# Two recurrences stepped in turns instead of in lockstep, with finer interleaving of side work, in a four-layer hybrid block

## The chip, the core and the metric

The program runs on one core of one Trainium2 chip. The metric is the device time of one execution in microseconds (us). A core has these engines, each with its own in-order instruction queue: TensorE (PE, matrix multiplication into PSUM), VectorE (DVE), ScalarE (ACT), GpSimd (POOL) and SyncE (SP, which here only issues DMA transfers). POOL also issues DMA transfers, the indirect ones, whose rows are chosen by indices in memory. An instruction that waits for another engine holds up everything behind it on its own engine. Nothing but such waits ties the engines together.

## What is computed

Input x is 4 sequences of 512 tokens of 128 features, all in float32. Four layers follow one another, each as `x = x + layer(layernorm(x))`:

```python
x = x + attn_a(layernorm(x), W)                   # 16 heads, scores |q.k|**2 with cumulated gates
x = x + ffn(layernorm(x), gate_w, bias, w1,w2,w3) # 8 experts, 2 per token, hidden 352
x = x + attn_b(layernorm(x), Wi, Wf, Wg, ..., Wo) # gated recurrence
x = x + ffn(layernorm(x), gate_w, bias, w1,w2,w3) # the same expert layer again
```

The recurrence layer projects x three times, runs a causal convolution of four taps over two of the projections, and then, per feature, scans over time; its output is normalized, gated and projected:

```python
f = sigmoid(conv(x @ Wf));  i = silu(conv(x @ Wi)) * (1 - f)
h_t = f_t * h_(t-1) + i_t
y = (h * rsqrt(mean(h*h) + eps) * g_norm * silu(x @ Wg)) @ Wo
```

The expert layer sends each token to its two best experts of eight: `silu(x @ w1[e]) * (x @ w3[e]) @ w2[e]`, weighted by the score.

## The kernel before

**Halves and stages.** After the attention the four sequences are worked as two halves q = 0, 1 of two sequences. The expert layer occurs twice, as generations gen = 1 and 2. Its tokens are sorted by expert into NS = 23 blocks of 128 places. So there are four expert stages (gen, q), in the order (1,0), (1,1), (2,0), (2,1), each a call of `blocks` (L982) with 28 iterations j. Block j is worked over several iterations: `first` (L1002) multiplies by w1 and w3 (tile ph, L1020; four matmuls), ACT takes silu (sl, L1027), DVE multiplies (h, L1028). Two iterations later `turn_and_second` (L1032) transposes h on PE (L1040) and ACT copies it (hT, L1053). Two iterations after that, PE multiplies by w2 (L1046) and ACT copies the result (yb, L1056). One iteration later `send` (L1058) writes the rows to memory at yg by an indirect DMA on POOL (L1059). Every fourth block `turn_x` (L990) transposes four blocks of fetched rows (px, L994; xT, L998). `fetch` (L962) brings rows eight blocks ahead: for stage (1,0) by SP, for the others by an indirect DMA on POOL (L970).

**Side work.** While one half is in the expert stage, the other half's connecting work is woven in. It is written as Python generators ("streams"); each `yield` ends a piece, and the block loop asks for the next piece at fixed points by `next(side)`. Since all engines are in-order, where a piece is asked for is where its instructions stand in every queue. Per iteration there are `points` such points: one after `first`, one at the end, and, if points > 2, one between the transposes and the w2 matmuls. A piece that issues a fetch reports "dma", and the rest of that iteration's points are dropped. `skip(n)` makes n empty pieces, to let time pass between a producer and its consumer. The list of stages, points and side streams is at L1229.

**The side streams.** Beside (1,0) runs the routing of half 1: `route` (L685) normalizes (stats, apply, turn), multiplies by the gate weights (pl, L747), finds the two best experts by a chain of small DVE operations (L773 to L806), counts places on PE (pp, L819 and L821), derives each token's place (L827 to L897) and inverts the list by counting matches (hit, L911; pi, L904). Then `begin` (L975) fetches the first eight blocks. Beside (1,1) and (2,0) runs `then` (L1212): `combine` (L1087) loads the expert results (yk) and adds them to x (L1102), `hgrn` (L1118) is the recurrence layer, then come `route` and `begin` for generation 2. Beside (2,1) only `combine` with the store of the output runs, and after the last block once more.

**Lockstep.** The two sequences of a half run through `combine` and `hgrn` under `both` (L220): each piece holds the same step of both sequences. `route` then normalizes both with tiles that hold the whole half.

**PSUM.** The tiles ph, px and all PE results of the side work come from one ring of three buffers (`ring`, L209), so an allocation waits until the third last one has been read. `busy` (L256) are matmuls without use that keep PE occupied; one stands before the last matmuls of each recurrence.

**The attention.** It runs in 16 steps (b, g) with the next two steps overlapped; POOL multiplies the scores by the decay (`faded`, L505, L514). From the middle on, the routing of half 0 is a side stream there too, at four points per step (`point`, L595); it ends with 16 indirect DMA writes of rows ("puts", L868) on POOL. What is left of it and `begin(1, 0)` is run off before the first block, one `busy` matmul to a piece.

## Time and profile before

| what | value |
|---|---|
| median of 14 runs | 636.79 us (633.35 to 649.2) |
| profiled execution, its own time | 633.89 us |
| span from first to last instruction of it | 632.2 us |
| mean granted TensorE clock | 0.921 |
| attention up to the first block's matmul | 0 to 255.3 us |
| stage (1,0), 23 blocks and routing of half 1 | 255.3 to 326.4 us |
| stage (1,1), with recurrence and routing of half 0 | 326.4 to 438.1 us |
| stage (2,0), with recurrence and routing of half 1 | 438.1 to 552.3 us |
| stage (2,1), with the sums and store of half 0 | 552.3 to about 616 us |
| last sums and store of half 1 | about 616 to 632.2 us |

How to read the profile: a page gives busy time by engine and, by groups, each line's instructions. The timeline lists instructions in order of time: start, busy time, engine, line, operation, tile written <- tiles read, count, and in square brackets the idle time of the engine before it and what released it. "PEclk" is the TensorE clock that was granted, in tenths. "remote" as releaser means that the profile could not tell which event ended the wait. Stage borders in the table are the starts of the first ph matmul of each stage in the timeline.

### The profile page before, as it was taken

The page shows a single profiled execution, that of the slowest core. Times are in us where ns is not written, and L with a number is a line of the kernel's source. Part 1 is how long each engine was busy: PE and PEld are TensorE (multiplying, and loading weights), DVE is VectorE, ACT ScalarE, POOL GpSimd, SP SyncE. Part 2 cuts the span into 40 slices and gives each one's busy share as a digit, 9 for nine tenths or more (in the row PEclk, how much of TensorE's full clock was granted, in tenths as well). Part 3 has the DMA queues.
Part 4 walks back from the last instruction along what each step waited for, and adds up shares of the span by engine and source line. Part 5 has one row for each costly group of instructions (what it writes and reads, how often), then busy time and mean ns, then how long its engine had stood idle before and what let it go on. Part 6 is the DMA issues. An engine that isn't in the chain of part 4 may idle for free.

```text
span 632.2 us, 11339 instructions
## 1 busy us (share of the span) xinstructions
PE 528.2 (84%) x4065; PEld 349.2 (55%) x4065; DVE 323.6 (51%) x772; ACT 281.9 (45%) x507; POOL 338.7 (54%) x487
## 2 busy tenths in 40 slices
PE   9899999999988978799886989774798978589890
PEld 4345555556554545567664567553556755457570
DVE  5527668796869754473216445640634655033211
ACT  2446776777755650443432434431343433134350
POOL 4645748566744696035674228347522733756651
PEclk9889999999988998999989979996897988699995
DMA  2360008993000001161122001301200121123113
GB/s 79 106 198 4 8 2 107 141 147 17 2 2 2 14 32 43 39 131 35 38 64 70 18 14 38 94 27 46 93 17 17 31 77 39 47 76 108 43 37 111
DMA packets 53974, 34.96 MB, mean 55 GB/s; under 512 B 18040, under 2 KB 49040, under 8 KB 53920
## 3 DMA queue, kind: packets, MB, share of 16 engines
q1 hardware_dynamic: 48052, 22.49, 18.1%
q0 software_dynamic: 5664, 11.70, 6.3%
q8 instruction: 34, 0.56, 0.4%
q14 instruction: 20, 0.16, 0.1%
q10 hardware_dynamic: 204, 0.05, 0.0%
HBM read 16.56 MB, written 17.66 MB: 54 GB/s over the span
## 4 chain that ended last, share of the span: by engine, by line
PE 53%; DVE 21%; issue 9%; POOL 7%; ACT 5%; DMA 3%; another core or an unknown queue 1%; SPq 1%; POOLq 0%; DVEq 0%; ACTq 0%
PE ph L1020 11%; PE pb L1046 7%; DVE p L444 6%; PE s L489 5%; PE busy L259 3%; PE pb L1040 3%; PE pd L473 3%; PE pd L470 3%; DVE h L1028 2%; PE od L525 2%; POOL yg L1059 2%; POOL p L514 2%; PE oo L530 1%; ACT sl L1027 1%; DMA yk<-yg 1%
## 5 line engine op out<-in xcount | busy, mean ns | idle before, releaser
L1059 POOL DMA_INDIRECT yg<-yb,xb x92 | 91.4, 994 | 130.1 <-ACT yb L1056 115.7
L1020 PE MATMUL ph<-w,xT 128*128 x368 | 133.6, 489 | 15.1 <-DVE xT L998 5.7
L514 POOL TENSOR_TENSOR p<-p,dec 128x256 f32<-128x256 f32 (+1 forms) x96 | 86.5, 918 | 68.5 <-ACT p L503 64.6
L1028 DVE SCALAR_TENSOR_TENSOR h<-ph,xb,sl 128x352 f32<-128x352 f32 x92 | 53.3, 580 | 130.1 <-ACT sl L1027 98.2
L503 ACT ACTIVATE p<-p,aeps 128x1024 f32<-128x1024 f32 (+1 forms) x96 | 94.1, 1004 | 38.4 <-DVE p L444 34.7
L444 DVE TENSOR_SCALAR p<-s 128x1024 int32<-128x1024 int32 (+1 forms) x96 | 95.2, 1035 | 23.4 <-PE s L489 23.4
L1046 PE MATMUL pb<-w2s,hT 128*128 x552 | 81.4, 286 | 14.3 <-remote 9.9
L1020 PEld LDWEIGHTS ph<-w,xT 128*128 128x128 f32 x368 | 66.5, 200 | 42.3 <-issue 9.0
L1027 ACT ACTIVATE sl<-ph,xb 128x352 f32<-128x352 f32 x92 | 51.5, 560 | 79.8 <-PE ph L1020 51.6
L1053 ACT COPY hT<-pb 128x384 f32<-128x384 f32 x92 | 44.1, 479 | 86.7 <-PE pb L1046 54.6
L1046 PEld LDWEIGHTS pb<-w2s,hT 128*128 128x128 f32 x552 | 72.8, 200 | 17.5 <-ACT yb L1056 13.1
L970 POOL DMA_INDIRECT xb<-xg,from x69 | 67.3, 976 | 25.0 <-issue 13.6
L489 PE MATMUL s<-qT,kT 32*128 32x256 f32 (+3 forms) x512 | 66.4, 476 | 9.8 <-DVE p L444 8.4
L1040 PE MATMUL pb<-ident,h 128*128 128x128 f32 x276 | 47.6, 283 | 7.3 <-ACT yb L1056 4.8
L489 PEld LDWEIGHTS s<-qT,kT 32*128 32x128 f32 x512 | 31.1, 185 | 34.9 <-DVE p L444 18.2
L1040 PEld LDWEIGHTS pb<-ident,h 128*128 128x128 f32 x276 | 35.5, 145 | 26.9 <-issue 13.1
L477 ACT ACTIVATE dec<-pd 128x1024 f32<-128x1024 f32 x32 | 32.5, 1023 | 27.0 <-PE pd L473 27.0
L998 DVE COPY xT<-px 128x512 f32<-128x512 f32 (+1 forms) x24 | 15.9, 660 | 33.8 <-PE px L994 30.5
L530 PE MATMUL oo<-p,vo 128*9 128x128 f32 x768 | 31.2, 279 | 0.0
L470 PE MATMUL pd<-negm,identb 128*128 128x512 bf16 x64 | 25.0, 390 | 5.5 <-DVE p L444 5.5
L461 POOL TENSOR_SCALAR kT<-kf,hsel 128x512 f32<-128x512 f32 x16 | 25.1, 1571 | 7.6 <-DVE kf L374 7.6
L525 PE MATMUL od<-p,v 128*9 128x128 f32 x512 | 24.8, 280 | 3.6 <-POOL p L514 3.6
(238 smaller groups left out, 694.2 us busy)
## 6 DMA issues: line engine op xcount, KB each, us to landing
xg<-zero SPq DMA_DIRECT2D x4, 1472.0 KB
yk<-yg SPq DMA_DIRECT2D x16, 256.0 KB
xg<-xk SPq DMA_DIRECT2D x6, 520.0 KB
w<-in_L_ffn_w_dram SPq DMA_DIRECT2D x2, 1408.0 KB
xb<-xg SPq DMA_DIRECT2D x23, 65.0 KB
yg<-yb,xb POOLq DMA_INDIRECT x92
xb<-xg,from POOLq DMA_INDIRECT x69
x<-in_L_attn_a_x_dram SPq DMA_DIRECT2D x4, 256.0 KB
```

The lines of the kernel that those rows point to most:

```text
L444: nc.vector.tensor_scalar(dst.bitcast(I32), src.bitcast(I32), 0x7FFFFFFF, None, ALU.bitwise_and)
L489: nc.tensor.matmul(sp[hh // 2][:, hh % 2, n : n + tn * P], kT[r, s * P : (s + 1) * P], qT[r, t0 * P : (t0 + tn) * P], start=True, stop=True,)
L503: nc.scalar.activation(pa, pa, AF.Square, bias=aeps)
L514: nc.gpsimd.tensor_tensor(d, d, e, ALU.mult)
L970: nc.gpsimd.indirect_dma_start(out=t, out_offset=None, in_=xg[gen, q], in_offset=bass.IndirectOffsetOnAxis(ap=gots[gen, q][1][:, j : j + 1 ...
L1020: nc.tensor.matmul(ph[:, w, 0:HID], xT[j], w13f[:, bass.ds(reg[j][0] + w * HID, HID)], start=True, stop=True,)
L1027: nc.scalar.activation(sl, ph[:, 0, 0:HID], AF.Silu, scale=score)
L1028: nc.vector.scalar_tensor_tensor(hs_[j % NHB][:, 0:HID], ph[:, 1, 0:HID], score, sl, ALU.mult, ALU.mult)
L1040: nc.tensor.transpose(bank[:, cols], hs_[jt % NHB][:, cols], ident)
L1046: nc.tensor.matmul(py, hT[js][:, k * P : (k + 1) * P], w2f[:, bass.ds(reg[js][1] + k * C, C)], start=(k == 0), stop=(k == len(FCH) - 1),)
L1053: nc.scalar.copy(hT[jt], bank[:, 0:HP])
L1059: put = nc.gpsimd.indirect_dma_start(out=yg[gen, q], out_offset=bass.IndirectOffsetOnAxis(ap=loaded[gen, q, j][:, C : C + 1].bitcast(I32), ...
```

## The change

The diff has these parts.

- `both` becomes `in_turns`: the two sequences' streams alternate piece by piece, the first one four pieces ahead. A stream now holds the sums, the recurrence and also the normalization for the routing (`route_norm`, with tiles of one sequence), so `route` starts behind both. The tiles xk are split by sequence.
- Four side points per iteration in the first three stages: the new one is inside `first`, between the w1 and w3 matmuls. The empty pieces are counted anew.
- `results` loads all four yk tiles at once; the sums come nine pieces later. `combine` only adds.
- The recurrence's steps are cut differently; the `busy` matmul before its last matmuls is dropped; ACT copies the mean squares before DVE reads them.
- In the routing the scores of both choices are taken in one multiply and one reduction, and ACT copies them into the four row tiles; SP writes the rows in four transfers.
- `begin` fetches two blocks per piece (in the slow form one, as before).
- In the last attention step DVE instead of POOL multiplies by the decay, and puts are issued two per point in the last two steps.

```diff
-    def both(*streams):
-        streams = list(streams)
+    def in_turns(first, second, lead):
+
+        for _ in range(lead):
+            next(first, None)
+            yield
+        streams = [second, first]
         while streams:
-            streams = [s for s in streams if next(s, END) is not END]
-            yield
+            for st in tuple(streams):
+                if next(st, END) is END:
+                    streams.remove(st)
+                else:
+                    yield
...
-        def faded(pas, rnd, dec):
+        def faded(pas, rnd, dec, eng):
...
-                nc.gpsimd.tensor_tensor(d, d, e, ALU.mult)
+                eng.tensor_tensor(d, d, e, ALU.mult)
...
-                if piece == "dma" and k % 2:
+                if piece == "dma" and (k % 2 or n + 1 >= NST):
                     next(second, None)
...
+                fader = nc.gpsimd if n + 1 < NST else nc.vector
+                faded(tiles[0], 0, decs[n], fader)
...
+    def route_norm(gen, q, i, early=False):
+
+        nm, xk = f"{gen}_{q}_{i}", xks[q]
+        xn = xk[0][i][:, :, 0:C]
+        yield from normed(xs[seqs(q)[i]], xn, f"r{nm}", 0 if early else 1)
+        xnT = rp.tile([P, NB, P], FP, tag=f"xnT{i}", name=f"xnT_{nm}")
+        turned(xnT.rearrange("p n t -> p (n t)"), xn, nm)
+        nc.scalar.copy(xk[1][i][:, :, 0:C], xn)
+        turned_rows[gen, q, i] = xnT
+        yield
+
+    turned_rows = {}
+
+    def first_done():
+        yield "first"
...
-        stats(0)
...
-            turn(1)
-            yield
+        nm, xk = f"{gen}_{q}", xks[q]
         yield
         pl = ring(f"pl_{nm}")[:, 0, 0 : HT * NE].rearrange("p (n e) -> p n e", e=NE)
         for n in range(HT):
-            nc.tensor.matmul(pl[:, n, :], xnT[:, n, :], gT, start=True, stop=True)
+            xnT = turned_rows[gen, q, n // NB]
+            nc.tensor.matmul(pl[:, n, :], xnT[:, n % NB, :], gT, start=True, stop=True)
...
-        yield
-        if not early:
-            yield
+        yield from skip(1 if early else 3)
...
-        for k, h in enumerate((hot1, hot2)):
-            nc.vector.tensor_tensor(tmp, sc, h, ALU.mult)
-            nc.vector.tensor_reduce(xk[k][:, :, C + 1], tmp, AX.X, ALU.add)
+        nc.vector.tensor_tensor(
+            both_tmp, sc.unsqueeze(1).to_broadcast([P, 2, HT, NE]), both_hot, ALU.mult
+        )
+        score = rp.tile([P, 2, 2, NB], FP, tag="score", name=f"score_{nm}")
+        nc.vector.tensor_reduce(
+            score.rearrange("p k i n -> p (k i n)"),
+            both_tmp.rearrange("p k n e -> p (k n) e"), AX.X, ALU.add,
+        )
+        for k in range(2):
+            for i in range(2):
+                nc.scalar.copy(xk[k][i][:, :, C + 1], score[:, k, i, :])
         for k in range(0 if early else 2):
-            nc.sync.dma_start(
-                out=xg[gen, q][k * HT * P : (k + 1) * HT * P, :].rearrange(
-                    "(n p) c -> p n c", p=P
-                ),
-                in_=xk[k],
-            )
-        yield from skip(1 if early else 4)
+            for i in range(2):
+                r = (2 * k + i) * T
+                nc.sync.dma_start(
+                    out=xg[gen, q][r : r + T, :].rearrange("(n p) c -> p n c", p=P),
+                    in_=xk[k][i],
+                )
+        yield from skip(1 if early else 3)
...
-        yield
+        yield from skip(1 if early else 2)
...
-            yield from skip(1 if m else 3)
+            yield from skip(1 if m else 2)
...
-        yield
+        yield from skip(2)
...
-            for j in range(2 * GR):
+            if not slow:
+                yield from skip(3)
+            for j in range(0, 2 * GR, 2):
                 fetch(gen, q, j)
+                if slow:
+                    yield "dma"
+                    yield
+                fetch(gen, q, j + 1)
                 yield "dma"
...
                 ph = ring(f"ph_{nm}_{j}")
+                dma = False
                 for w in range(2):
+                    if w and points > 3:
+                        dma = next(side, None) == "dma"
                     nc.tensor.matmul(
...
+                return dma
...
-                if j < NS:
-                    first(j)
+                dma = j < NS and first(j)
                 if j % GR == 1 and j // GR + 1 < groups:
                     turn_x(j // GR + 1)
-                dma = next(side, None) == "dma"
+                dma = dma or next(side, None) == "dma"
...
+        def results(gen, q, got):
+
+            yk = {}
+            for i in range(2):
+                for k in range(2):
+                    t = fp1.tile([P, NB, C], FP, tag=f"yk{k}{i}", name=f"yk{k}_{gen}_{q}_{i}")
+                    r = (2 * k + i) * T
+                    ld = nc.sync.dma_start(
+                        out=t, in_=yg[gen, q][r : r + T, :].rearrange("(p n) c -> p n c", n=NB)
+                    )
+                    behind(ld, got[2], "every result is in its row")
+                    yk[k, i] = t
+            return yk
+
+        def combine(q, yk, i, store=False):
+            b = seqs(q)[i]
             for k in range(2):
...
-                nc.vector.tensor_tensor(xs[b], xs[b], yk[k], ALU.add)
-                if not store:
+                nc.vector.tensor_tensor(xs[b], xs[b], yk[k, i], ALU.add)
+                if k or not store:
...
             yield from normed(xs[b], xn, f"h{b}", 1)
-            yield from skip(2)
...
-            pf = ring(f"pf_{b}")
...
+            pr = ring(f"pr_{b}")[:, 0, :]
+            nc.tensor.matmul(pr, hw[:, 0, :], xnT[:, PAD:], start=True, stop=True)
+            nc.scalar.copy(raw[:, PAD:], pr)
+            yield
+            pf = ring(f"pf_{b}")[:, 0, :]
+            for k in range(CK):
                 nc.tensor.matmul(
-                    pf[:, 0, :], wfk[:, k, :], xnT[:, k : k + T], start=(k == 0), stop=False
+                    pf, wfk[:, k, :], xnT[:, k : k + T], start=(k == 0), stop=(k == CK - 1)
                 )
-            nc.scalar.copy(raw[:, PAD:], pf[:, 1, :])
-            yield
...
+            nc.scalar.activation(om, pf, AF.Tanh, scale=0.5)
             nc.vector.tensor_scalar(acc, raw[:, 0:T], cw[:, 0, 0:1], None, ALU.mult)
-            yield
-            nc.scalar.activation(fg, om, AF.Copy, bias=0.5, scale=0.5)
-            nc.vector.scalar_tensor_tensor(
-                acc, raw[:, 1 : 1 + T], cw[:, 0, 1:2], acc, ALU.mult, ALU.add
-            )
-            yield
-            for k in range(2, CK):
+
+            def tap(k):
                 nc.vector.scalar_tensor_tensor(
                     acc, raw[:, k : k + T], cw[:, 0, k : k + 1], acc, ALU.mult, ALU.add
                 )
-                if k == 2:
-                    pg = ring(f"pg_{b}")[:, 0, :]
-                    nc.tensor.matmul(pg, hw[:, 2, :], xnT[:, PAD:], start=True, stop=True)
-                else:
-                    nc.scalar.activation(sg, pg, AF.Silu)
+
+            yield
+            tap(1)
+            pg = ring(f"pg_{b}")[:, 0, :]
+            nc.tensor.matmul(pg, hw[:, 2, :], xnT[:, PAD:], start=True, stop=True)
+            nc.scalar.activation(fg, om, AF.Copy, bias=0.5, scale=0.5)
+            nc.scalar.activation(sg, pg, AF.Silu)
+            yield
+            for k in range(2, CK):
+                tap(k)
+                if k == CK - 1:
+                    nc.scalar.activation(si, acc, AF.Silu)
                 yield
-            nc.scalar.activation(si, acc, AF.Silu)
             nc.vector.scalar_tensor_tensor(si, om, -1.0, si, ALU.add, ALU.mult)
             yield
             nc.vector.tensor_tensor_scan(o, fg, si, 0.0, ALU.mult, ALU.add)
             nc.scalar.activation(o2, o, AF.Square)
             yield
             nc.vector.scalar_tensor_tensor(sg, o, gn, sg, ALU.mult, ALU.mult)
-            yield from skip(4)
+            yield from skip(2)
             pss = ring(f"pss_{b}")
-            busy(pss[:, 1, :], 1)
             for n in range(NB):
...
+            rr = hp.tile([P, NB], FP, tag="rr", name=f"rr_{b}", bufs=2)
+            nc.scalar.copy(rr, pss[:, 0, 0:NB])
             nc.scalar.copy(ym, pss[:, 1, :].rearrange("p (n c) -> p n c", c=C))
-
-            rr = hp.tile([P, NB], FP, tag="rr", name=f"rr_{b}", bufs=2)
-            nc.vector.tensor_scalar(rr, pss[:, 0, 0:NB], 0.25 / C, RMS_EPS, ALU.mult, ALU.add)
+            yield from skip(2)
+
+            nc.vector.tensor_scalar(rr, rr, 0.25 / C, RMS_EPS, ALU.mult, ALU.add)
             nc.gpsimd.tensor_tensor(rr, rr, mhalf[:, 0:1].to_broadcast([P, NB]), ALU.pow)
-            yield
-            yield
+            yield from skip(2)
...
+        rest = attention(lambda: chain(
+            route_norm(1, 0, 0, True), first_done(), route_norm(1, 0, 1, True),
+            route(1, 0, gots[1, 0], early=True),
+        ))
+        begin, blocks, results, combine = expert_pools()
         hgrn = recurrence_pools()
 
-        def then(gen, q, go_on):
-
-            got = gots[gen, q]
-            b0, b1 = seqs(q)
-            if go_on:
-                yield from both(
-                    chain(combine(gen, q, got, 0, False), hgrn(b0)),
-                    chain(combine(gen, q, got, 1, False), hgrn(b1)),
+        def then(gen, q):
+
+            yk = results(gen, q, gots[gen, q])
+            yield from skip(9)
+            if gen == 1:
+                yield from in_turns(
+                    *(
+                        chain(combine(q, yk, i), hgrn(b), route_norm(gen + 1, q, i))
+                        for i, b in enumerate(seqs(q))
+                    ),
+                    4,
                 )
                 yield from route(gen + 1, q, gots[gen + 1, q])
                 yield from begin(gen + 1, q)
             else:
-                yield from combine(gen, q, got, 0, True)
-                yield from combine(gen, q, got, 1, True)
+                for i in range(2):
+                    yield from combine(q, yk, i, True)
 
 
         rest = chain(rest, begin(1, 0))
         for stage, points, side in (
-            ((1, 0), 2, chain(route(1, 1, gots[1, 1]), begin(1, 1, True))),
-            ((1, 1), 3, then(1, 0, True)),
-            ((2, 0), 3, then(1, 1, True)),
-            ((2, 1), 2, then(2, 0, False)),
+            ((1, 0), 4, chain(
+                in_turns(route_norm(1, 1, 0), route_norm(1, 1, 1), 2),
+                route(1, 1, gots[1, 1]), begin(1, 1, True),
+            )),
+            ((1, 1), 4, then(1, 0)),
+            ((2, 0), 4, then(1, 1)),
+            ((2, 1), 2, then(2, 0)),
```

## The prediction

> **What bounds the kernel now.** I read the page first, then busy time by stage, then PE's timeline and beside it those of DVE, ACT and POOL, last the chain.
>
> ```profile
> span 632.2 us, 11339 instructions
> PE 528.2 (84%) x4065; PEld 349.2 (55%) x4065; DVE 323.6 (51%) x772; ACT 281.9 (45%) x507; POOL 338.7 (54%) x487
> ```
>
> PE is the busiest, but its 104 us of idleness are not spread evenly. The table by stretch (PE, weight loads, DVE, ACT, POOL, clock) cuts stage (1,1) at its recurrence part, routing part and end:
>
> ```profile
> 326.40:380.40 54.00, 45.36 (x194) 29.66 (x195) 26.18 (x65) 19.11 (x41) 21.15 (x29) 0.91 0.14 40
> 380.40:419.90 39.50, 30.90 (x193) 22.24 (x192) 24.20 (x87) 14.28 (x36) 19.69 (x29) 1.00 0.21 56
> 419.90:438.10 18.20, 9.97 (x63) 8.24 (x61) 1.86 (x3) 4.87 (x14) 12.84 (x18) 0.78 0.16 43
> ```
>
> No engine is full there: PE waits in its own order. Its timeline shows where, and what a block costs when it doesn't:
>
> ```profile
> 342.07 1.00 PE L253 MATMUL ps_h<-ident,xn_h 128*128 128x128 f32 x4 [2.32 <-DVE xn_h L243]
> 344.76 1.95 PE L1136 MATMUL pf<-xnT_h,hw 128*128 128x512 f32 x2
> ...
> 361.77 1.35 PE L1020 MATMUL ph<-w,xT 128*128 x4
> 362.96 0.49 PE L1040 MATMUL pb<-ident,h 128*128 128x128 f32 x3
> 363.29 0.83 PE L1046 MATMUL pb<-w2s,hT 128*128 x6
> 363.96 1.35 PE L1020 MATMUL ph<-w,xT 128*128 x4
> ...
> 368.49 2.03 PE L259 MATMUL pss<-ident 128*128 128x512 f32 x2 [2.75 <-DVE h L1028]
> ...
> 404.59 0.21 PE L819 MATMUL pp<-hot,upto_b 128*128 128x72 bf16 x1 [2.43 <-DVE hot L801]
> ...
> 414.08 0.27 PE L904 MATMUL pi<-at,hit 128*128 128x46 bf16 x4 [1.72 <-DVE hit L911]
> ...
> 434.78 1.65 PE L1046 MATMUL pb<-w2s,hT 128*128 x6 [5.45 <-remote]
> ```
>
> From ph to ph a block takes 363.96 - 361.77 = 2.19 us. Twice the lockstep recurrences make PE wait: for both norms (2.32, then 0.68) and for DVE's long run before the last matmuls (2.75). Behind such waits PE runs at half clock (1.95 us for two pf matmuls that take 1.02 at 349.01; the clock record has 0.5 for 3.4 us from 344.7 and 6.8 us from 368.6). The routing waits come from the DVE chain. The wait at 434.78 falls into POOL's unbroken run of fetches and sends (420.5 to 433.0); ACT's copy before it waited 5.73 us "remote".
>
> **The change, part by part.** Sums are against the profiled 633.89 us (span 632.2, 1.7 around it); the median is 2.9 higher, and the same difference is applied to it.
>
> *Recurrence part, (1,1) and (2,0).* I count the pieces: nine empty ones, then the sums from the end of j=2, turns in j=5 and 6, pf in j=6 and 7, last matmuls in j=10 and 11. Until j=5 I leave the 11.5 us of before (326.44 to 337.94). Blocks 5 to 10: six of 2.19 = 13.1, two px of 0.44 = 0.9. PE side work: two turns of 0.44, two raw of 0.86, two pf of 8 x 0.43 = 3.44, two pg of 0.86, and one set of last matmuls (1.50 + 1.93 at half clock, 1.77 at full): 13.0. The two useless pss matmul pairs (0.86 each) are gone. New waits, walked through DVE's order: the first turn stands one iteration behind its norm, and DVE has h, two sums and the statistics (1.2) ahead of it, with POOL's 0.23 + 1.04 between: 1.7 us. The first raw matmul takes the ring buffer of h(5), 0.6; the second turn 0.6. From j=7 on taps, scan and products (DVE at most 4.0 us in an iteration) lie beside pf (3.44) of the other sequence: no wait. Sum 11.5 + 13.1 + 0.9 + 13.0 + 2.9 = 41.4, and 1.8 for the second sequence's last matmuls: 43.2 against 54.0: -10.8 per stage.
>
> *Routing part of the same stages.* Before, eleven iterations at three pieces; now it must fit into j=12 to 21 at four. POOL: a fetch and a send cost 2.55 us per iteration (1.28 each by their spacing), and norm powers (1.04 each) of both sequences fall into j=11 to 14, so the second norm's factors come late: the second turn waits 4.0, the first 0.9 (before: 0.84 and 0.16). The chain from mx to the second best takes 6.24 us (398.26 to 404.5) with one h inside; pp now stands 1.75 iterations behind its start instead of 2.7, wait 3.5 (before 2.43 + 1.37). The first counts wait 3.4 + 0.9 for place, at and hit (DVE 7.8 us; before 1.72 + 1.39). Walked through with these, 40.0 to 42.7 us against 39.5, the upper end with half clock behind the 4.0: I take +3. The one multiply and reduction for the scores save DVE about 0.2, the four ACT copies cost some 0.8 to 1.4 (nearest row: ACT's 128x64 silu, 0.35), in front of hT, which has two iterations of slack. Two more SP transfers (0.5 each to issue) wait for nothing and have 15 us before the first fetch. Free, while their cover lasts: ACT's small copy of the mean squares (ACT had been idle for 5.16 us at that place; without cover 0.3 four times), POOL's numbering of four tiles for two (0.39 each, beside busy pieces), and all four yk loads at once on SP, where nothing stands behind them until the routing's stores.
>
> *Ends of these stages.* Eight fetches still go out within j=22 to 24, now in pairs, so POOL runs them with fewer sends between: one to two more indirect DMAs (1.28 each) before it stops for a yb: +1.5 per stage. If the wait is not tied to POOL's run, 0.
>
> *Stage (1,0).* Two points become four: the routing is done by j=7 instead of j=13, where blocks are short on PE (j=2, 3: 1.52). The DVE chain of some 15 us now stands over six iterations. Walked through, pp waits 2.4, the ring 1.4, counts 4.8, against 2.0 in all before: +6, less what an earlier first turn gives. I take +5, bounds 0 (the row 259.32, a wait of 1.65 at the start, goes) and +9 (half clock twice).
>
> *Attention's end.*
>
> ```profile
> 229.31 1.42 POOL L514 TENSOR_TENSOR p<-p,dec 128x256 f32<-128x256 f32 x2
> ...
> 234.46 3.85 POOL L514 TENSOR_TENSOR p<-p,dec 128x512 f32<-128x512 f32 x4
> ```
>
> Six puts stand between and in front of these; PE waited 2.96 and 0.61 for them and then ran at half clock. On DVE (nearest row: x<-x,yb 128x512, 0.68) the six multiplications take about 3 us and end near 234.2 instead of 238.3. But the puts, still 16 x 1.27 us on POOL, then run unbroken, and a long run is where "remote" waits stand. One busy piece fewer (0.86). Bounds -6 and -1; I take -4.
>
> *End.* The second pair of yk loads was issued at 624.13, behind the first store:
>
> ```profile
> 619.59 0.80 SPq L1094 DMA_DIRECT2D yk<-yg  x2
> 623.69 0.39 SPq L1106 DMA_DIRECT2D out_dram<-x  x1
> 624.13 0.99 SPq L1094 DMA_DIRECT2D yk<-yg  x2
> ```
>
> Now four go at once. At the first pair's rate (2.63 us) four land by 624.9 instead of 627.05; at best the sums follow each other at 623.7. Between -2.2 and -3.4: -2.5. Stage (2,1) keeps two points: 0 (+-2).
>
> Sum: 2 x (-10.8 + 3 + 1.5) - 4 + 5 - 2.5 = -14.1; with the median 636.79 - 14.1, about 623.
>
> **A rule against it.** The clock record goes to 0.5 behind idle times of 2.3 and 2.75 us, though not behind 2.43 at 402. The Trainium skill (TensorE: Matmul & The Clock Gate, section "HAM oscillation — how this bites in real kernels") asks for no idle gaps above some 3.4 us. By that rule the waits of 1.7 to 3.5 us that I expect would keep full clock and the estimate would be some 3 us lower; by the trace's rows they don't all keep it, and the trace decides. The same skill (SBUF — State Buffer, section "Who interferes with whom") says that a DVE operation with two SBUF inputs and a GpSimd operation reading SBUF exclude each other, which speaks against the decay on DVE beside puts. In this trace the DVE sum at 226.21 took 0.68 beside a put (225.72), as elsewhere, so I add nothing; by the page's rule up to six operations could each wait for a put of 0.96, about 6 us, and the attention's gain would be gone.
>
> **Rivals.** (a) *Larger gain:* the waits at the ends of (1,1) and (2,0) (2.0 + 5.45 and 2.28 + 4.43, with half clock from 430.0 and 542.6 for 13.7 us each, about 6 lost) depend on how fetches and sends meet the last blocks; if pairing them moves POOL's run behind PE's last blocks, up to 27 us go besides: 596 to 610. For it: the last blocks take only 1.0 us each on PE. Against: the run starts at the same iteration. (b) *Nothing:* turns win the recurrence part but what it leaves is paid back by the routing: the gains are 2 x 10.8 + 4 + 2.5 - 2 x 1.5 = 25.1; if each of the three routing parts costs 7.3 to 9.4 us instead of 3, 3 and 5, the time is 633.6 to 640. (c) *Slower:* the routing decides alone. PE is in-order, and a side matmul now stands between w1 and w3, so a late DVE result holds back h, sl's partner and the ring at once, at half clock behind. Above 9.4 us per routing part: 640 to 650. For it: DVE work of 15 us plus h (0.58) and xT over six iterations of 2.19 fills DVE nearly; against: at (1,1) the same chain already made PE wait 8 us before and cost that little. That the change doesn't take place is excluded: the order is written out by hand.
>
> **How the numbers follow.** A measurement tells 0.5% (3.2 us) from no change. Main case, -6 to -22: 0.60. (a): 0.12. (b), within 0.5%: 0.10. (c): 0.18. So faster 0.72, same 0.10, slower 0.18. The main case's own range is 612 to 631. For 8 in 10 the range takes half of (a) and a third of (c): 606 to 642.
>
> **What would show it.** Right: no pss<-ident rows; no PE wait above 2 us from j=5 to 11; that part near 43 us; POOL without p<-p,dec behind 230; x sums at the end within 2 us of each other. Wrong: PE waits at pp, pi or the second turn above 5 us each; (1,0) longer than 80 us; waits "remote" in the recurrence part, as the two streams' fetches now meet PE's shorter blocks; or attention's end behind 252.

## The result and the profile after

The changed kernel took 660.12 us (median of 10 runs, 656.03 to 671.81) against 638.37 us of the kernel before (median of 47). The ratio is 1.0395 with a 95% interval of 1.0362 to 1.0428: slower, where 623 us had been predicted. The profiled execution took 663.67 us, 29.8 more than the one before. First the head of the page of the changed kernel:

```profile
span 662.0 us, 11363 instructions
PE 544.7 (82%) x4055; PEld 358.2 (54%) x4055; DVE 326.9 (49%) x770; ACT 284.5 (43%) x527; POOL 335.6 (51%) x485
```

PE has 10 matmuls fewer than before but is busy 16.5 us longer: nearly the same work at a lower clock (mean granted clock 0.884 against 0.921). The table by stretch (PE, weight loads, DVE, ACT, POOL, clock) cuts stage (1,1) of the changed kernel at blocks 11 and 21, as the prediction cut the one before:

```profile
350.39:393.67 43.28, 38.57 (x174) 25.10 (x174) 22.42 (x54) 18.37 (x40) 21.66 (x27) 0.96 0.18 52
393.67:443.70 50.03, 39.99 (x209) 30.24 (x207) 28.06 (x94) 16.02 (x43) 20.11 (x29) 0.80 0.17 42
443.70:461.57 17.87, 11.01 (x66) 8.63 (x63) 2.13 (x5) 4.87 (x14) 11.13 (x15) 0.79 0.14 38
```

The recurrence part takes 43.28 us, where 54.00 stood before and 43.2 had been predicted; of the 43.2, 1.8 us were for the second sequence's last matmuls, which now stand behind the cut (at 396.1). But the routing part grew from 39.50 to 50.03, and the stage is as long as it was. PE's timeline of the changed kernel shows two waits of the attention (for p, the absolute values that DVE takes of the scores), then those of the routing in (1,0) and in (1,1):

```profile
202.63 1.22 PE L501 MATMUL s<-qT,kT 32*128 32x256 f32 x4 [2.17 <-DVE p L456]
222.42 1.22 PE L501 MATMUL s<-qT,kT 32*128 32x256 f32 x4 [2.50 <-DVE p L456]
...
287.05 0.24 PE L800 MATMUL pp<-hot,upto_b 128*128 128x72 bf16 x1 [3.38 <-DVE hot L774]
298.26 0.34 PE L885 MATMUL pi<-at,hit 128*128 128x46 bf16 x4 [3.31 <-DVE hit L892]
...
411.33 1.39 PE L265 MATMUL ps<-ident,xk 128*128 128x128 f32 x4 [4.26 <-DVE xk L255]
429.17 1.13 PE L271 MATMUL pp<-ident 128*128 128x512 f32 x2 [2.45 <-DVE h L1018]
439.11 0.27 PE L885 MATMUL pi<-at,hit 128*128 128x46 bf16 x4 [1.60 <-DVE hit L892]
441.93 0.33 PE L885 MATMUL pi<-at,hit 128*128 128x46 bf16 x4 [1.40 <-DVE hit L892]
```

The clock record has 13.7 us of 0.5 with each of the waits of 2.17, 2.50 and 4.26 us; they begin in the wait, at 201.75, 222.24 and 409.97. DVE's timeline has waits whose end the profile can't place, in the attention's end; POOL's unbroken run of 13 puts stands there (233.3 to 249.4 us):

```profile
246.79 1.23 DVE L456 TENSOR_SCALAR p<-s 128x1024 int32<-128x1024 int32 x1 [10.08 <-remote]
251.74 1.22 DVE L456 TENSOR_SCALAR p<-s 128x1024 int32<-128x1024 int32 x1 [3.72 <-remote]
```

The kernels of the experiments ran later, where all was faster: the kernel before took 606 to 611 us there. So the pair was run there once more (second column of differences). The parts are cut at the first ph matmul of each stage, in us, from the profiled executions:

| part | before | after | predicted | difference | difference, second pair |
|---|---|---|---|---|---|
| attention, to the first block | 255.3 | 270.6 | -4 | +15.3 | -2.5 |
| (1,0) | 71.1 | 79.8 | +5 | +8.7 | +13.6 |
| (1,1) | 111.6 | 111.2 | -6.3 | -0.4 | +1.7 |
| (2,0) | 114.2 | 115.5 | -6.3 | +1.3 | +4.3 |
| (2,1) and the end | 79.9 | 84.9 | -2.5 | +5.0 | -3.2 |
| sum | 632.2 | 662.0 | -14.1 | +29.8 | +13.9 |

The two columns share the losses in (1,0) and the missing gains in (1,1) and (2,0). They do not share the attention's +15.3 (51.2 us of it at half clock against 20.5 before, in the second pair 20.5 in both) and the +5.0 of the last stage. Three of the traces below, marked *, are of executions 1.6 to 2.1% above the fastest of their kernel, so that their parts are upper values.

### The profile page after: what moved, and what is told of

It is laid out like the page before. It is cut to its first block, busy times and chain, and to the rows that moved or that the text cites. A ratio compares the mean times of both kernels' runs of the same rounds, so it can differ in the third digit from the quotient of the medians.

```text
span 662.0 us, 11363 instructions
## 1 busy us (share of the span) xinstructions
PE 544.7 (82%) x4055; PEld 358.2 (54%) x4055; DVE 326.9 (49%) x770; ACT 284.5 (43%) x527; POOL 335.6 (51%) x485
## 4 chain that ended last, share of the span: by engine, by line
PE 59%; DVE 17%; issue 8%; another core or an unknown queue 5%; ACT 5%; POOL 4%; DMA 2%; SPq 0%; POOLq 0%; ACTq 0%; DVEq 0%
PE ph L1010 13%; PE pb L1037 7%; PE s L501 7%; DVE p L456 5%; PE busy L271 3%; PE pd L485 3%; PE pb L1031 3%; PE pd L482 3%; DVE h L1018 2%; PE oo L542 2%; PE od L537 2%; PE pf L1132 2%; ACT sl L1017 2%; PE pl L722 2%
## 5 line engine op out<-in xcount | busy, mean ns | idle before, releaser
L1010 PE MATMUL ph<-w,xT 128*128 x368 | 147.8, 523 | 30.7 <-DVE xT L985 13.2
L526 POOL TENSOR_TENSOR p<-p,dec 128x256 f32<-128x256 f32 (+1 forms) x90 | 81.2, 919 | 76.2 <-ACT p L515 70.1
L1010 PEld LDWEIGHTS ph<-w,xT 128*128 128x128 f32 x368 | 70.7, 216 | 57.1 <-issue 18.3
L1017 ACT ACTIVATE sl<-ph,xb 128x352 f32<-128x352 f32 x92 | 51.2, 558 | 103.4 <-PE ph L1010 53.3
L501 PE MATMUL s<-qT,kT 32*128 32x256 f32 (+3 forms) x512 | 70.0, 488 | 15.0 <-DVE p L456 11.5
L1037 PEld LDWEIGHTS pb<-w2s,hT 128*128 128x128 f32 x552 | 74.7, 205 | 4.3 <-ACT yb L1047 2.4
L1044 ACT COPY hT<-pb 128x384 f32<-128x384 f32 x92 | 43.9, 477 | 60.0 <-PE pb L1037 42.6
L501 PEld LDWEIGHTS s<-qT,kT 32*128 32x128 f32 x512 | 33.0, 191 | 41.6 <-DVE p L456 19.9
L1031 PEld LDWEIGHTS pb<-ident,h 128*128 128x128 f32 x276 | 38.1, 152 | 26.3 <-issue 16.1
L1031 PE MATMUL pb<-ident,h 128*128 128x128 f32 x276 | 49.2, 291 | 3.5 <-ACT yb L1047 3.5
L542 PE MATMUL oo<-p,vo 128*9 128x128 f32 x768 | 33.0, 278 | 4.5 <-issue 4.5
L1047 ACT COPY yb<-pb 128x128 f32<-128x128 f32 x92 | 25.2, 274 | 11.1 <-PE px L981 6.7
```

Of the source, the lines that this page charges most:

```text
L501: nc.tensor.matmul(sp[hh // 2][:, hh % 2, n : n + tn * P], kT[r, s * P : (s + 1) * P], qT[r, t0 * P : (t0 + tn) * P], start=True, stop=True,)
L526: eng.tensor_tensor(d, d, e, ALU.mult)
L1010: nc.tensor.matmul(ph[:, w, 0:HID], xT[j], w13f[:, bass.ds(reg[j][0] + w * HID, HID)], start=True, stop=True,)
L1017: nc.scalar.activation(sl, ph[:, 0, 0:HID], AF.Silu, scale=score)
L1031: nc.tensor.transpose(bank[:, cols], hs_[jt % NHB][:, cols], ident)
L1037: nc.tensor.matmul(py, hT[js][:, k * P : (k + 1) * P], w2f[:, bass.ds(reg[js][1] + k * C, C)], start=(k == 0), stop=(k == len(FCH) - 1),)
```

## The experiments

All sixteen variants in one table: parts in us from the profiled execution, the median, and the ratio to the kernel before with its interval.

| kernel | attention | (1,0) | (1,1) | (2,0) | (2,1), end | median | ratio |
|---|---|---|---|---|---|---|---|
| before_again | 253.4 | 65.4 | 103.3 | 110.2 | 79.3 | 612.47 | 1.0117 (1.0058 to 1.0176) |
| after_again | 250.9 | 79.0 | 105.0 | 114.5 | 76.1 | 630.77 | 1.0454 (1.0360 to 1.0547) |
| attn_as_before | 256.5 | 76.9 | 106.3 | 112.4 | 73.5 | 627.38 | 1.0321 (1.0241 to 1.0401) |
| fades_on_pool* | 267.2 | 78.8 | 105.0 | 114.2 | 73.3 | 636.94 | 1.0361 (1.0274 to 1.0449) |
| one_piece_earlier | 249.5 | 77.3 | 107.0 | 112.0 | 73.9 | 623.80 | 1.0221 (1.0121 to 1.0320) |
| two_points_10* | 256.7 | 76.1 | 107.7 | 112.3 | 75.7 | 623.64 | 1.0145 (1.0066 to 1.0224) |
| kept_busy | 258.4 | 73.8 | 105.7 | 115.3 | 77.2 | 632.79 | 1.0420 (1.0316 to 1.0523) |
| lockstep_3 | 260.1 | 76.3 | 105.6 | 112.2 | 73.9 | 628.97 | 1.0401 (1.0332 to 1.0469) |
| ten_as_before | 256.5 | 68.8 | 108.8 | 113.6 | 76.0 | 629.07 | 1.0364 (1.0280 to 1.0449) |
| turns_mended | 249.5 | 70.4 | 104.3 | 109.7 | 74.7 | 613.02 | 1.0105 (1.0007 to 1.0203) |
| lockstep_mended | 254.4 | 70.1 | 105.7 | 113.5 | 76.2 | 618.52 | 1.0161 (1.0085 to 1.0237) |
| turns_dense | 247.6 | 71.6 | 99.7 | 109.9 | 75.2 | 607.71 | 0.9992 (0.9947 to 1.0036) |
| dense_stores_act | 249.9 | 69.3 | 103.1 | 107.1 | 77.0 | 607.53 | 1.0018 (0.9980 to 1.0055) |
| dense_stores_turn | 251.8 | 68.8 | 99.4 | 108.6 | 75.9 | 605.72 | 0.9932 (0.9898 to 0.9966) |
| two_parts_alone* | 252.9 | 65.9 | 100.7 | 105.4 | 76.6 | 602.76 | 0.9854 (0.9792 to 0.9916) |
| lockstep_dense | 254.4 | 67.8 | 105.1 | 113.0 | 75.0 | 615.66 | 1.0125 (1.0083 to 1.0167) |

The first row is a control, and it limits all others: the same kernel against itself came out 1.0117. A ratio within some 1.2% of 1 is no sure difference here. The attention of after_again, two_points_10, kept_busy, lockstep_3 and ten_as_before has the same instructions up to the last few us, and took 250.9 to 260.1; by part, too, only differences above 5 us or so, or seen in several kernels, are used.

### The pair on the same chip

> The kernel before once more, for a trace on the same chip as the three beside it. On the first chip its stage (1,1) took 111.6 us, of it 42.45 from block 5 to 11 and 39.5 from block 11 to 21, and waits called remote of 3.7 to 5.7 us stood at 314, 434 and 548 us. In the traces of the four variants of the changed kernel no wait is called remote. If these waits belong to the chip, this trace has none either, and its stages (2,0) and (2,1) start some 5 us earlier each.

> The changed kernel once more, on the same chip as the kernel before. If the waits called remote, which follow POOL's long runs of indirect DMAs (231.7 to 249.5, 448.7 to 471.2, 566.4 to 591.4 us), belong to the chip, the ratio is lower here: 1.015 to 1.025 instead of 1.0395, with stage starts (blocks 0 to 5 of (1,1), (2,0), (2,1)) near 8 to 11 us instead of 13.7, 19.0 and 21.0. If they belong to the kernel, the ratio stays near 1.04.

No wait called remote stands in either trace, nor in any of the other fourteen. So they belong to where or when the first pair ran (the runs can't tell these apart), together with a kernel: in the first pair the changed kernel had more of them (67 us over DVE and ACT) than the one before (28 us over PE, ACT and DVE). But the ratio did not fall with them as expected: 1.0454, or 630.77 / 612.47 = 1.030 against the control. The loss is there without the remote waits. By the table by stretch of both kernels (before_again first), for (1,0) and (1,1):

```profile
253.41:318.79 65.38, 60.38 (x376) 46.47 (x376) 28.89 (x78) 31.39 (x76) 31.11 (x49) 1.00 0.27 62
318.79:422.07 103.28, 88.17 (x444) 63.07 (x444) 52.51 (x154) 38.60 (x91) 49.81 (x70) 0.88 0.18 48
```

```profile
250.93:329.96 79.03, 68.31 (x371) 50.87 (x372) 30.26 (x80) 30.93 (x78) 31.12 (x51) 0.87 0.23 51
329.96:434.94 104.98, 87.08 (x439) 62.05 (x439) 52.82 (x152) 39.07 (x97) 49.70 (x68) 0.88 0.18 47
```

In (1,0) DVE is busy 1.4 us longer and PE has five matmuls fewer, but PE idles 10.7 us instead of 5.0 and runs at 0.87 instead of full clock. In (1,1) all engines do nearly the same in nearly the same time.

### The attention's end

attn_as_before has all three edits, fades_on_pool the first alone, one_piece_earlier the last alone:

```diff
-                fader = nc.gpsimd if n + 1 < NST else nc.vector
+                fader = nc.gpsimd
...
-                if piece == "dma" and (k % 2 or n + 1 >= NST):
+                if piece == "dma" and k % 2:
...
         nm, xk = f"{gen}_{q}", xks[q]
-        yield
+        if not early:
+            yield
         pl = ring(f"pl_{nm}")[:, 0, 0 : HT * NE].rearrange("p (n e) -> p n e", e=NE)
```

> The changed kernel with its attention's end as before: decays of the last step on POOL again, two puts only at every second point, and the first stage's routing back at its earlier count of pieces (the change has one empty piece more between the second sequence's turn and the gate matmuls). The first block of (1,0) started at 270.6 us in the changed kernel and at 255.3 in the one before. Theory: nothing else in the change reaches that part, so the block starts at 255 to 257 again and the whole is 14 to 16 us faster than the changed kernel, about 1.6% slower than the kernel before. Rival: the new tiles and the normalization in two parts cost there too; then the block starts at 262 or later and the gain is below 9 us.

> The changed kernel with one thing undone: the last step's six multiplications by the decays stand on POOL again, between the puts. Theory A, the unbroken run of 13 puts (231.7 to 249.5 us) is what delays PE's signals to DVE and ACT (10.08 and 10.76 us idle there): the run is broken into pieces again, the waits called remote at 239 to 247 go, and the first block starts some 5 to 9 us earlier than 270.6. Rival B, the loss is all in the two waits of 2.17 and 2.50 us at 200 and 220 and the half clock behind them: the block starts within 2 us of 270.6. Rival C, DVE is the better place, as the prediction had it: the block starts 1 to 6 us later.

> The changed kernel with one thing undone: the empty piece between the turn of the second sequence and the gate matmuls of the first stage's routing is taken out, so that each later piece stands one place earlier in the attention, as before the change. Theory: the waits for the absolute values at 200.45 (2.17 us) and 219.91 (2.50 us), each with 13.7 us of half clock behind it, came only from where these pieces fall on DVE; they go, and by 231 us the kernel is some 10 us earlier (8 to 12), and so is the first block (270.6 before). Rival: the waits are there at any place of the pieces; the block starts within 2 us of 270.6.

attn_as_before starts its first block at 256.5 us, as expected by the first theory; but here the changed kernel itself starts it at 250.9 to 260.1, so nothing is saved by going back on all three together, and the whole stays 3.2% slower. With the empty piece gone both waits for p are gone, in every kernel that has this edit, and with the fades on DVE the first block starts at 247.6 to 254.4 us (seven kernels, mean 251.0). With the piece it starts at 250.9 to 260.1 (five kernels, mean 256.5). So by these means one empty piece cost some 5.5 us, an estimate, not the 10 expected: the two groups overlap and differ in other parts as well, and one_piece_earlier, which differs in the piece alone, is at 249.5 only 1.5 us below after_again. What the piece costs goes with the time at half clock. In after_again, PE's timeline has

```profile
202.38 0.70 PE L501 MATMUL s<-qT,kT 32*128 32x256 f32 x4 [2.17 <-DVE p L456]
217.32 0.70 PE L501 MATMUL s<-qT,kT 32*128 32x256 f32 x4 [2.67 <-DVE p L456]
```

and half clock only behind the second (10.2 us from 218.4). In two_points_10 the same two waits (2.17 and 2.50) each come with 13.7 us of it. Up to the first block the five kernels had 20.5, 33.0, 37.5, 37.5 and 44.4 us at half clock, in the order of their times; from the first and the last of them, an estimate: (260.1 - 250.9) / (44.4 - 20.5) = 0.4 us lost per us at half clock.

The fades: with them on POOL, PE waits for them (in before_again; 4.06 us in attn_as_before, 3.67 in fades_on_pool). On DVE no kernel has that wait:

```profile
235.99 0.60 PE L525 MATMUL od<-p,v 128*9 128x128 f32 x4 [4.09 <-POOL p L514]
```

In fades_on_pool the fades stand between the puts again (groups of 4, 4 and 5 from 238.3 to 260.1) and no wait is called remote; but none is beside unbroken runs either, so it could not tell the theory of the unbroken run. That theory fell otherwise: two_points_10 has 13 puts from 233.2 to 249.7 and one_piece_earlier 42 indirect DMAs from 537.0 to 590.5 in one run, and no wait beside them is called remote. A long run alone does not delay PE's signals. What else it takes was not found: what the first pair met did not come again, so breaking the runs by other work could not be tried where it would tell.

### Stage (1,0)

two_points_10 changes `((1, 0), 4, chain(` to 2; ten_as_before does that and puts both normalizations in the old order:

```diff
-            ((1, 0), 4, chain(
-                in_turns(route_norm(1, 1, 0), route_norm(1, 1, 1), 2),
+            ((1, 0), 2, chain(
+                norms_in_step(1, 1),
```

> The changed kernel with two side points per block in stage (1,0), as before, instead of four. The stage took 79.8 us in the changed kernel (270.6 to 350.4) and 71.1 before. Theory: the loss is the routing drawn together into seven blocks, with waits of 3.38 at pp and 3.31 at pi and 17 us of half clock; with two points it takes 70 to 73 us, and the whole is 7 to 10 us faster than the changed kernel. Rival: the norms in two parts and the smaller stores cost it; then the stage stays above 77.

> The changed kernel with the side work of stage (1,0) in the old order: two points per block, both statistics, both applications and then both turns of the normalization (the small stores of the rows and the score copies stay as changed). On one chip the stage took 65.4 us in the kernel before and 79.0 in the changed one; with two points alone 76.1, with a wait of 3.02 at the second turn, half clock for 13.7 us behind it and a wait of 3.20 for a load. Theory: normalization in turns and the four points together cost the 13.6; the stage takes 65 to 68 us and the whole is 11 to 14 us faster than the changed kernel, equal to the kernel before within 1%. Rival: the four smaller stores and the copies hold up SP's loads; the stage stays above 70.

Two points alone left (1,0) at 76.1 or somewhat less: the second turn came too close behind its norm (3.02 us, and 13.7 us of half clock). With the old order as well it took 68.8 us instead of 79.0 (and 67.8 to 71.6 in the six later kernels with this order): 10.2 of the 13.6 us come from the weave. Its whole did not follow (1.0364, where within 1% was expected): its attention took 5.6 us longer than after_again's and (1,1) 3.8 longer, with the same instructions. What is left in (1,0) is a wait for a load. SP's and PE's timelines of ten_as_before:

```profile
277.38 2.30 SPq L805 DMA_DIRECT2D xg<-xk  x4
279.73 6.93 SPq L962 DMA_DIRECT2D xb<-xg  x9
```

```profile
286.08 0.33 PE L995 MATMUL px<-ident,xb 128*128 128x128 f32 x1 [2.83 <-DMA xb<-xg]
```

The four stores wait for the score copies on ACT, and the loads of later blocks stand behind them on SP. In before_again the stores go out 17.9 us behind the stage's start, here 20.9, and PE waited for a load 0.53 there against 2.83 here. dense_stores_act, on top of turns_dense (below), lets ACT issue the stores:

```diff
-                nc.sync.dma_start(
+                nc.scalar.dma_start(
                     out=xg[gen, q][r : r + T, :].rearrange("(n p) c -> p n c", p=P),
```

> The dense turns, with the routing's four row stores issued from ACT's queue instead of SP's. In stage (1,0) SP's loads of later rows stand behind these stores, which wait for ACT's four score copies; PE waited 3.60 us for a load in block 10 (0.53 before the change), with 6.8 us of half clock behind. Theory: SP, in order, is what holds the loads; they go out as soon as their buffers are there, the wait goes, (1,0) takes 65 to 68 us instead of 71.6, and the whole is 3 to 6 us faster than the dense turns, 0.985 to 0.995 of the kernel before. Rival: the transfers themselves are in the way on the queues; the wait stays above 2 us and (1,0) above 70.

The wait for the load goes (also in the two later kernels with this edit), and (1,0) falls from 71.6 to 69.3, where 65 to 68 had been expected (PE now waits 1.82 us for ACT's yb in its place); the other stages moved by up to 3.4 us either way, and the whole is unchanged. That SP held the loads is shown; that it is worth 3 to 6 us is not.

### The half clock in the routing

kept_busy puts `busy` in front of the second turn (8), pp (7 for 1) and pi (5 for 1).

> The changed kernel with useless 128x512 transposes more on PE, ahead of what it waits for: 8 before the second sequence's turn of the routing in (1,1) and (2,0) (it waited 4.26 and 6.43 us), 6 more before pp (2.45 to 3.49), 4 more before pi (1.6 to 3.3), 0.43 us each. Theory A: half of the routing's loss is the half clock behind these waits (27 us of 0.5 in the routing part of (1,1)); with it gone blocks 11 to 21 take 43 to 46 us instead of 50, and the whole is 8 to 14 us faster than the changed kernel. Rival B: the stage's length is set by the chain of the second sequence through DVE and POOL, not by PE's rate; then blocks come earlier but wait longer, and the stage stays within 2 us. Rival C: the useless work itself delays; 2 to 8 us slower.

The expectation had a wrong price: one `busy` is two matmuls of 0.43 us, so the pieces are twice as long as stated. PE's timeline of kept_busy in (1,1):

```profile
385.38 7.03 PE L273 MATMUL ps<-ident 128*128 128x512 f32 x16
405.01 7.67 PE L273 MATMUL pp<-ident 128*128 128x512 f32 x14 [3.50 <-DVE h L1020]
417.21 4.45 PE L273 MATMUL pi<-ident 128*128 128x512 f32 x10
```

Against after_again, half clock went from 25.4 to 3.4 us in (1,1), from 39.5 to 19.0 in (2,0) and from 20.5 to 3.4 in (1,0), where only pp and pi are preceded by more. (1,0) gained 5.2 us (79.0 to 73.8); (1,1) and (2,0) did not change (105.7 and 115.3), and blocks 11 to 21 of (1,1) took 53.1 us where 43 to 46 had been expected. The pieces added there are 18 of 0.86, 15.5 us; the wait of 3.50 stayed, ahead of pp's pieces, and in after_again the waits at the turn and at pi had been 4.27 and 1.75. That this useless work used up what the clock gave is argued from these numbers; rival B, a chain that sets the stage's length, would leave the stages equal as well. The whole is equal.

### Turns or lockstep

lockstep_3 takes the turn-taking, with its fourth point, out of the changed kernel. turns_mended has (1,0) in the old order, no empty piece in the first routing, and earlier fetches:

```diff
             count(m)
-        yield from skip(2)
+        yield
...
-            if not slow:
-                yield from skip(3)
-            for j in range(0, 2 * GR, 2):
+            for j in range(2 * GR):
                 fetch(gen, q, j)
-                if slow:
-                    yield "dma"
-                    yield
-                fetch(gen, q, j + 1)
                 yield "dma"
                 if slow:
                     yield
```

lockstep_mended is the same with

```diff
-                yield from in_turns(
+                yield from both(
...
-            ((1, 1), 4, then(1, 0)),
-            ((2, 0), 4, then(1, 1)),
+            ((1, 1), 3, then(1, 0)),
+            ((2, 0), 3, then(1, 1)),
```

> The changed kernel with the turn-taking alone undone in (1,1) and (2,0): both sequences step in lockstep again, at three points per block; norms in two parts, single px buffers, pairs of fetches, attention's end and stage (1,0) as changed. Prediction's theory: the turns save 10.8 us per stage in the recurrence part and the routing pays little; lockstep is then 10 to 20 us slower than the changed kernel. Rival, from the trace of the changed kernel: what sets the stage's length is the last sum of the second sequence, which ended 56.0 us behind the start of (1,1) against 53.7 before, so the turns won nothing for the chain behind it; lockstep is then equal or up to 10 us faster than the changed kernel, with its last sums at 52 to 56 us and its block 11 at 50 or later.

> As the kernel with (1,0) in the old order, and two more things undone: the empty piece in the first stage's routing goes, and in (1,1) and (2,0) the fetches for the next stage start three to four pieces earlier, one per piece, as before (the rows to fetch were known 95 to 105 us behind the stage's start, against 92 and 99 before). Theory: what is left is the turn-taking itself with four points; (1,1) takes 102 to 105 us and (2,0) 110 to 114, against 103.3 and 110.2 before, and the whole is within 1% of the kernel before: turn-taking wins nothing. The prediction's theory: with the mishaps mended, the saving of 10.8 us in each recurrence part shows, and the whole is 2 to 3% faster than before.

> The same as the mended turns, but both sequences in lockstep at three points, as before, so that the pair differs in the turn-taking alone. Theory, the last sum of the second sequence sets the routing: equal to the mended turns within 4 us. The prediction's theory: 15 to 20 us slower than the mended turns.

lockstep_3 and after_again are equal (628.97 and 630.77; (1,1) and (2,0) together 217.8 and 219.5). The mended pair differs by 5.5 us, (1,1) and (2,0) by 1.4 and 3.8: a little more than the 4 us allowed, far from 15 to 20, and the intervals of the two ratios overlap. turns_mended is 1.1% above the kernel before, so a gain over it doesn't show.

What turn-taking does inside (1,1) shows when the stage is cut at blocks 11 and 21, lockstep_3 first, then after_again:

```profile
336.34:387.67 51.33, 44.46 (x189) 30.88 (x190) 24.44 (x58) 19.68 (x43) 23.64 (x31) 0.87 0.15 45
387.67:430.75 43.08, 34.88 (x192) 24.71 (x191) 25.08 (x90) 14.88 (x40) 17.78 (x27) 0.88 0.21 49
```

```profile
329.96:372.35 42.39, 39.08 (x174) 25.93 (x174) 22.62 (x54) 18.27 (x40) 21.95 (x29) 0.92 0.18 55
372.35:422.30 49.95, 38.71 (x208) 28.69 (x207) 28.07 (x94) 15.93 (x43) 19.79 (x29) 0.83 0.18 42
```

Turns bring block 11 earlier by 8.9 us, and the routing behind it takes 6.9 longer (16 matmuls, 1.8 us, only moved across the cut). The same holds in (2,0), -9.8 and +9.5, and in the mended pair, -9.8 and +8.3 in (1,1) and -12.0 and +8.2 in (2,0). So there is a saving (7 to 10 us without the moved matmuls; 10.8 had been predicted against the kernel before), and most or all of it is paid back in the same stage. In lockstep_3 the routing parts are 43.1 and 43.5 us against 36.9 and 37.3 in before_again: some 6 us more stand there through the other edits, while block 11 comes 4.2 and 4.7 us earlier than in before_again.

Why, the DVE timelines of (1,1) show: the last sum of the second sequence and the list of rows to fetch, in the first pair, before and after:

```profile
378.11 2.39 DVE L1195 SCALAR_TENSOR_TENSOR x<-ym,rr,x 128x128 f32<-128x128 f32 x8
...
419.53 0.18 DVE L928 TENSOR_TENSOR from<-part,pi 128x23 int32<-128x23 f32 x1
```

```profile
405.55 1.14 DVE L1183 SCALAR_TENSOR_TENSOR x<-ym,rr,x 128x128 f32<-128x128 f32 x4 [1.08 <-POOL rr L1180]
...
447.72 0.18 DVE L909 TENSOR_TENSOR from<-part,pi 128x23 int32<-128x23 f32 x1
```

From the stage's start (326.44 and 350.39) the sums are complete after 54.1 us before the change and 56.3 after it, and the list comes after 93.1 and 97.3. The routing needs both sequences. In turns, a sequence gets two of four pieces of a block, in lockstep all three; the second sequence ends no earlier. What came earlier is the blocks: block 11 started 10.7 us sooner, and ten blocks were left for a routing whose chain was not shorter. PE then waited at the turn, at pp and at pi.

That can be tried: let the recurrence have six points in blocks 2 to 10 and the routing three, as before.

```diff
+                more = points > 3 and 2 <= j <= 10
+                if more:
+                    next(side, None)
-                dma = j < NS and first(j)
+                dma = j < NS and first(j, more)
...
-                    if w and points > 3:
+                    if w and more:
...
+                if more:
+                    next(side, None)
                 if turns:
...
-            yield from skip(9)
+            yield from skip(12 if gen == 1 else 9)
```

> The mended turns with the recurrences denser: six points per block in blocks 2 to 10 of (1,1) and (2,0), then three as before. The second sequence's last sum then stands in block 10 instead of 13, and the routing gets back the eleven blocks that it had before the change. Theory, the chain of the second sequence sets the stage: its last sum comes at 48 to 52 us behind the start instead of 55, the rows to fetch are known at 88 to 92, the waits at turn, pp and pi shrink to those before, and each of the two stages is 3 to 8 us shorter than with the mended turns. Rival: PE waits in the recurrence for DVE what it gains, the last sum stays at 54 to 56, and the stages stay within 2 us.

DVE's and PE's timelines of turns_dense in (1,1), which starts at 319.25:

```profile
366.95 1.14 DVE L1197 SCALAR_TENSOR_TENSOR x<-ym,rr,x 128x128 f32<-128x128 f32 x4 [1.09 <-POOL rr L1194]
...
407.81 0.18 DVE L924 TENSOR_TENSOR from<-part,pi 128x23 int32<-128x23 f32 x1
```

```profile
331.03 1.46 PE L265 MATMUL ps_h<-ident,xn_h 128*128 128x128 f32 x4 [3.50 <-DVE xn_h L255]
...
371.75 1.40 PE L265 MATMUL ps<-ident,xk 128*128 128x128 f32 x4 [2.11 <-DVE xk L255]
390.39 0.21 PE L815 MATMUL pp<-hot,upto_b 128*128 128x72 bf16 x1 [0.85 <-DVE hot L789]
```

The sums are complete after 48.8 us, the list after 88.6, the wait at the turn is 2.11 instead of 4.26 and at pp 0.85; the stage takes 99.7 us instead of 104.3. In (2,0) there was no gain (109.9 after 109.7), though the last sums were complete after 58.2 us instead of 63.5: its results were added later (first sums 16.2 us behind the start against 13.3), block 11 came 7.8 us later, and the list only 0.6 earlier (98.0 against 98.6). So earlier sums alone do not shorten a stage. The gain of 4.6 in (1,1) lies below the limit set above for one trace, but it recurs: the three dense kernels with turns took 99.7, 103.1 and 99.4 there, the eight with four points 104.3 to 108.8. The kernel before, in lockstep, took 103.3, and 100.7 in two_parts_alone, whose edits do not touch this stage; and the whole of turns_dense equals the kernel before.

> As the dense turns with stores from ACT, but both sequences in lockstep, at four points in blocks 2 to 10 (so that the last sums come at about the same block) and three after. What is open: whether the gain of the dense turns is the turn-taking or the density. If the turns carry it, lockstep leaves (1,1) at 103 to 106 us and (2,0) at 110 to 114; if the density, both come within 2 us of the dense turns (99.7 and 109.9).

```profile
335.49 1.24 PE L271 MATMUL ps_h<-ident,xn_h 128*128 128x128 f32 x4 [4.98 <-DVE xn_h L261]
357.50 1.05 PE L1183 MATMUL pss<-ones,o 128*128 128x1 f32 x8 [2.47 <-ACT o L1176]
373.43 1.16 PE L271 MATMUL ps<-ident,xk 128*128 128x128 f32 x4 [3.78 <-DVE xk L261]
```

In lockstep, at a density that completes the sums at the same time (48.2 us; the list at 89.5), PE waits longer for each pair of results, as these rows of its PE timeline show. Block 11 starts 60.9 us behind the stage's start instead of 46.8, and the stages take 105.1 and 113.0 us against 99.7 and 109.9, or 103.1 and 107.1 in dense_stores_act; the medians of lockstep_dense and dense_stores_act differ by 8.1 us, and the intervals of their ratios do not overlap. So at this density turns do fill PE better than lockstep; against the kernel before no gain is sure.

dense_stores_turn adds one empty piece before the second turn in (1,1) and (2,0):

```diff
         yield from normed(xs[seqs(q)[i]], xn, f"r{nm}", 0 if early else 1)
+        yield from skip(1 if gen == 2 and i else 0)
```

> As before it, and the second sequence's turn of the routing one piece later in (1,1) and (2,0). It waited 2.11 us in both, with 10.2 us of half clock behind it. Theory: wait and half clock go; the stages shorten by 1 to 4 us each. Rival: the chain through DVE sets the end and the routing is only one piece later; within 1.5 us per stage.

The wait did not go (1.79 and 2.32 us). (1,1) took 99.4 instead of 103.1 us, (2,0) 108.6 instead of 107.1. Half clock fell from 20.6 to 11.1 us in (1,1), and went from 20.4 to 23.3 in (2,0). It ends at 0.9932, 1.8 us below dense_stores_act by the medians: no more than a hint.

### Two parts alone

The kernel before with only DVE's fades in the last step and, at the end:

```diff
-        run(then(2, 1, False))
+        last = [combine(2, 1, gots[2, 1], i, True) for i in range(2)]
+        for st in last:
+            next(st)
+        for st in last:
+            run(st)
```

> The kernel before with two parts of the change alone: the last step's six multiplications by the decays on DVE instead of POOL, and all four result loads at the end issued at once. The prediction gave them -4 (bounds -6 and -1) and -2.5 (bounds -3.4 and -2.2). Theory: both hold by themselves, and what made the attention's end late in the changed kernel came from the other changes in it (one piece later in the routing, and POOL's unbroken run on the first chip); the first block starts 3 to 7 us earlier than 253.4, the end is 2 to 3 us shorter, and the whole is 0.985 to 0.995 of the kernel before. Rival: the fades on DVE win nothing; within 2 us of before up to the first block.

This has the lowest median, 602.76 us, ratio 0.9854; that is 1.5% below 1, little more than the 1.2% of the control, so a gain is likely but not sure. From block 21 of (2,1) to the end it takes 22.4 us instead of 25.5: -3.1, as in the changed kernel (22.8). PE's wait of 4.09 for POOL's fades is gone, but the first block starts at 252.9 against 253.4: 10.2 us of half clock from 209.1 stand in this trace and not in the control's, so the rival's "within 2 us" holds and the fades' worth isn't settled. The rest, 7.4 us in (1,1) and (2,0), lies in instructions that were not edited, and is not claimed.

## Why the prediction was wrong

The step that failed is the price of the routing: +3 us in each of (1,1) and (2,0) and +5 in (1,0), so that -6.3 of the recurrence part's -10.8 was to remain. It measured +10.5, +10.7 and +8.7 us, and +13.0, +15.7 and +13.6 in the second pair. Between the predicted -14.1 and the measured +29.8 lie 43.9 us; the attention has 19.3 of them, the largest share, which did not come again in the second pair (28.0 between forecast and measurement there, 27.2 of it in these three stages).

- **Recurrence part, -10.8 per stage: about right in size, but not a gain.** The stage's start to block 11 took 43.28 us; without the 1.8 that moved behind this cut, 41.4 had been worked out, so the saving is 8.9 on the same matmuls. In (2,0) it was 49.0 against 54.7, the first blocks of it held up (blocks 0 to 5 took 19.0 against 11.3); in the second pair 42.4 against 55.5 and 47.7 against 62.2. Which block stands beside a step is not when the step is done: the sums that the routing needs were complete after 56.3 us, 2.2 later than before (1.0 later in the second pair). turns_dense, which brings them 5.1 us earlier than turns_mended (48.8 against 53.9), has a (1,1) that is 4.6 us shorter; its (2,0), with sums 5.3 earlier, is not shorter.
- **Routing, +3 per stage: it measured +10.5 in (1,1) and +10.7 in (2,0)**, or 8.7 and 8.9 without the 1.8 us of the second sequence's last matmuls. In (1,1) the waits were named well (turn 4.0 predicted, 4.26; pp 3.5, 2.45; counts 3.4 + 0.9, 1.60 + 1.40); in (2,0) the turn waited 6.43. The prediction let half clock count behind the turn alone, at its upper end; it stood behind pp and the counts as well (3.4 and 6.8 us in (1,1)), and the clock was 0.80 in that part. Half clock is not all of it: kept_busy removed 22.0 us of it from (1,1), at the price of useless matmuls, and the stage stayed. That turn-taking itself moves its saving into this part is shown by lockstep_3 and the mended pair; what else adds the other 6 us there was not taken apart. Rival (c) had this mechanism, from a limit of 9.4 us per part; the second pair's parts, 50.0 against 36.9 and 53.0 against 37.3, lie above it even with the 1.8 taken off, those of the first pair, so taken, do not.
- **(1,0), +5 with bounds of 0 and +9: it measured +8.7 and +13.6.** The signs (pp 3.38, pi 3.31 + 1.01) are near the walk (2.4, 4.8). The upper bound took half clock for the routing's waits twice and did not hold: in the second pair the stage ran at 0.87.
- **Attention's end, -4: it measured +15.3 and -2.5.** The fades' wait went as predicted. Not seen was that the routing's stream had become one piece longer, so that its DVE pieces met the absolute values (5.5 us in the mean over later runs). In the first pair came waits called remote of 13.8 us beside the unbroken puts; the prediction named them as a danger and put no price on it. How the +15.3 divides between these waits and the half clock (51.2 us against 20.5), and what the remote waits are, stays open.
- **Ends of the stages, +1.5 each: not settled.** From block 21 to the next stage's start, (1,1) and (2,0) took 0.3 and 3.8 us less in the first pair, 1.8 and 3.0 more in the second. The starts behind them had no price: in the first pair blocks 0 to 5 of (2,0) and (2,1) took 7.7 and 9.8 us more, with remote waits; in the second both began faster (11.0 us against 17.7 and 17.2). The kernels with the earlier fetches were not better at these places.
- **Final end, -2.5: right**, -2.6, -2.7 and, alone, -3.1.
- **Rivals.** (a) needed the remote waits to go; they grew. (b) and (c) were of one mechanism, and (c), priced at 640 to 650, came nearest; the measured 660 lies above it, with the attention's loss and the held-up starts on top. Of the signs of being wrong, the turn in (2,0) (6.43), remote waits in the recurrence part and the attention's end (270.6) appeared.
- **The clock rule.** The Trainium skill (TensorE: Matmul & The Clock Gate, section "HAM oscillation — how this bites in real kernels") warns of idle gaps above some 3.4 us. Here waits of 2.17, 2.50 and 2.67 us came with 10.2 or 13.7 us of half clock, beginning in them or just behind, and one of 2.17 did not; the measurement decides. The prediction followed the rows and let some of them count, but too few.
